# A transformer block with routed experts on one core: a new order of all sequences' steps, first weights on two queues, and a unit matrix transposed before the first operands

## The chip, the cores and the metric

The kernel runs on one core of a Trainium2 chip. A core has TensorE (matrix products, PE in the profile, with its weight loads as PEld), VectorE (DVE), ScalarE (ACT), GpSimd (POOL) and SyncE (SP), each with a queue of its own that is worked in order, and 16 DMA engines. The metric is the device time of one execution in microseconds, the median of the runs; lower is better.

## The reference: what is computed

All values are 32-bit floats. There are 16 sequences of 256 tokens of width 256. A conditioning vector per sequence is turned into a shift, then attention with 16 heads of width 64 runs, then eight experts each take the 512 tokens with the highest gate value.

```python
shift = silu(t) @ W_ada.T + b_ada
h = ln(x, ln1_g, ln1_b) + shift
qkv = (h @ Wqkv.T).reshape(b, n, 3, H, HD)
q = ln(qkv[:, :, 0].transpose(0, 2, 1, 3), qn_g, qn_b)
k = ln(qkv[:, :, 1].transpose(0, 2, 1, 3), kn_g, kn_b)
v = qkv[:, :, 2].transpose(0, 2, 1, 3)
attn = softmax(einsum('bhnd,bhmd->bhnm', q, k) / sqrt(HD))
x = x + einsum('bhnm,bhmd->bhnd', attn, v).transpose(0, 2, 1, 3).reshape(b, n, H * HD) @ Wout.T
tok = x.reshape(-1, d)
gate = softmax(tok @ Wgate.T)
vals, idx = top_k(gate.T, bs // E)
g = ln(tok[idx_flat], mlp_g, mlp_b).reshape(k_cap, E, d)
y = gelu(einsum('ked,ehd->keh', g, fc1s) + b1s)
y = (einsum('keh,edh->ked', y, fc2s) + b2s) * w[..., None]
tok = tok.at[idx_flat].add(y.reshape(-1, d))
```

## The kernel before, in words

**Tiles.** Tokens lie on the 128 partitions, two tiles to a sequence (t = 0, 1). A 32-bit matmul is two passes of TensorE, a transpose (a matmul against the unit matrix `ident`) is one, and the profile counts passes. The work of a sequence is cut into classes whose methods are *steps*:

- `First`: statistics of x on VectorE, a power of −1/2 on GpSimd (L82), normalised x (L500), four transposes (`ph`, L524), and the copy to `hT` with gain and shift on ScalarE (L532).
- `Group(g, t)`: 512 columns of the projection (`pm`, L556, two matmuls). Groups 0 and 1 make q, 2 and 3 make k, 4 and 5 make v. q and k groups then go through square (ScalarE, L569), sum (VectorE, L573), power (GpSimd), scale (VectorE, L589), four transposes (`pq`, L598) and a copy (ScalarE, L610); a v group is only copied (L565).
- `Quad(d)`: four heads, in two pairs i = 0, 1. Scores of a pair (`sc`, L631: four matmuls with 64 rows of operands), row maxima (VectorE, L638), exponentials with sums (ScalarE, L647), reciprocal, scaling (GpSimd, L658), transposes (`pp`, L667), copies to `prT` (VectorE L675 or ScalarE L677), the product with v (`po`, L685: four matmuls for a pair, each writing 64 rows of the result), and after both pairs one copy of `po` to `oT` (VectorE, L697).
- `Tail(t)`: the output projection (`pw`, L709, eight matmuls), residual, store, normalisation, the gate's logits (`pg` L731, `pl` L742).

**Routing and experts.** After the gates, a search of 30 steps finds each expert's threshold bit by bit: VectorE compares (L826), TensorE counts with two tiny matmuls (`pc`, L856 and L857), VectorE decides (L872). Then tokens get places (`pplace`), lists are made with one-hot matmuls (`pls`, L985), rows are gathered by indirect DMA, and 16 jobs (eight experts, two halves) run two matrix products each (L1032, L1048) and add their rows to the output by indirect DMA. The search for the first half runs while the last sequence's attention is under way.

**Buffers.** [...] three for tag `mm` (`pa`, `ph`, `pm`, `pq`, `pg` and small ones), four for `sc` (scores and the transposed exponentials), one for `po` (products, output projection, gate logits). In SBUF, `hT`, `qT`, `kT`, `v` and `oT` have two buffers each (the default of the pool, L426), x has five, `pr` and `prT` eight.

**What sets the order.** An engine works its instructions in the order in which the program issues them, and here that order is written out by hand as numbers. `at(places, *steps)` gives every step of every object a *place*; the whole plan is sorted by place and run once. Places of a sequence in the middle are those of `STEADY` plus b times `PERIOD`; `START` and `END` hold other places for the first and last sequences; `SHIFT`, `CENTER`, `GATES`, `TURN`, `SEARCH`, `PLACE`, `LIST`, `UP`, `DOWN` hold those of single steps. Places act by their order alone: nothing waits for a time. Of a step's instructions each goes to its own engine's queue. What follows the first job is issued by loops (`Job`, `lay_out`) outside the plan.

**The start.** SP issues the loads in this order: x of sequence 0, `wa`, the blocks of `wq` for groups 0, 2, 4, x of sequence 1, blocks 1, 3, 5, then `wo` (L465 to L472). `vec`, `cT` and `wg` go over ScalarE's queue. Blocks 0 to 3 are centred in place by VectorE before use (`center`, L478 to L480, twice per block).

Of the kernel before, what the change touches and what calls it, by code (L numbers as in the profile page):

```python
# [9 lines left out]
F32 = mybir.dt.float32  # L10
# [8 lines left out]
P = 128  # L19
# [24 lines left out]
def kernel(  # L44
# [35 lines left out]
    def rsqrt(dst, src):  # L80
# [59 lines left out]
    PERIOD = 55.74  # L140
    STEADY = dict(
        first=((-86.48, -78.84, -74.84), (-85.13, -84.23, -75.17), (-73.21, -72.54)),
        group={
            (0, 0): (-51.60, -49.66, -48.99, -47.86, -45.60, -40.27, -37.29),
            (0, 1): (-49.89, -47.94, -45.00, -43.96, -42.22, -32.07, -31.41),
            (1, 0): (-24.39, -22.45, -21.77, -20.73, -18.77, -16.60, -15.29),
            (1, 1): (-26.11, -24.16, -23.49, -22.45, -20.71, -11.67, -10.68),
            (2, 0): (-39.83, -37.89, -37.22, -36.18, -34.31, -31.64, -30.60),
            (2, 1): (-38.12, -34.68, -33.12, -32.08, -28.64, -21.80, -20.95),
            (3, 0): (-7.64, -4.23, -3.56, -1.89, 2.62, 3.70, 6.68),  # L150
            (3, 1): (-9.35, -7.41, -6.74, -3.55, -1.19, 9.31, 9.98),
            (4, 0): (-53.91, -51.13),
            (4, 1): (-42.15, -39.94),
            (5, 0): (-11.07, -8.97),
            (5, 1): (-4.61, -2.66),
        },
        quad={
            (0, 0): (0.00, 4.89, 9.75),
            (0, 0, 0): (1.42, 3.71, 5.16, 7.57, 8.23),
            (0, 0, 1): (2.02, 2.81, 6.07, 8.00, 8.67),  # L160
            (0, 1): (-1.04, 3.21, 12.60),
            (0, 1, 0): (0.23, 1.01, 6.97, 8.87, 9.54),
            (0, 1, 1): (0.83, 1.91, 3.48, 8.44, 9.26),
            (1, 0): (10.73, 16.50, 25.41),
            (1, 0, 0): (12.00, 12.78, 17.68, 19.77, 22.02),
            (1, 0, 1): (14.11, 14.89, 16.77, 19.33, 21.66),
            (1, 1): (11.77, 21.34, 28.26),
            (1, 1, 0): (15.91, 19.26, 22.51, 24.97, 25.74),
            (1, 1, 1): (14.71, 20.16, 21.61, 24.53, 25.95),
            (2, 0): (26.39, 30.55, 40.23),  # L170
            (2, 0, 0): (28.29, 29.37, 30.82, 33.50, 35.62),
            (2, 0, 1): (27.69, 28.47, 31.73, 34.37, 35.60),
            (2, 1): (27.43, 36.22, 43.08),
            (2, 1, 0): (29.48, 30.27, 37.58, 39.57, 40.24),
            (2, 1, 1): (28.88, 33.89, 36.67, 38.70, 39.86),
            (3, 0): (41.21, 45.50, 53.71),
            (3, 0, 0): (42.48, 43.26, 46.67, 50.69, 51.36),
            (3, 0, 1): (43.08, 44.16, 45.77, 50.25, 50.92),
            (3, 1): (42.25, 50.11, 56.57),
            (3, 1, 0): (44.90, 45.87, 51.28, 53.28, 53.94),  # L180
            (3, 1, 1): (45.58, 48.93, 50.38, 52.84, 53.67),
        },
        out=(15.31, 30.96, 44.30, 59.03),
        tail=((75.94, 79.63, 83.54, 87.30, 84.99, 86.37, 88.80, 89.54), (90.54, 94.23, 95.33, 101.91, 95.74, 99.41, 105.55, 106.29)),
# [3 lines left out]
            first=((-103.767, -95.871, -91.909), (-97.063, -91.499, -84.828), (-64.982, -60.069)),  # L188
            group={
                (0, 0): (-56.803, -54.747, -51.852, -46.726, -46.286, -40.948, -38.071),  # L190
                (0, 1): (-55.655, -51.889, -46.959, -45.652, -42.360, -35.597, -33.112),
                (1, 0): (-26.197, -24.462, -20.588, -19.209, -14.535, -13.716, -13.269),
                (1, 1): (-32.516, -25.059, -24.852, -21.979, -18.889, -16.671, -15.729),
                (2, 0): (-47.233, -46.547, -44.993, -44.096, -39.234, -33.671, -28.238),
                (2, 1): (-45.275, -40.554, -40.280, -39.778, -36.553, -34.586, -30.446),
                (3, 0): (-12.610, -11.185, -8.404, -8.124, -5.996, 0.834, 3.448),
                (3, 1): (-13.363, -12.739, -11.605, -8.322, -7.543, 0.483, 2.162),
                (4, 0): (-58.243, -54.205),
                (4, 1): (-38.500, -37.978),
                (5, 0): (-9.805, -0.465),  # L200
                (5, 1): (-0.114, 0.811),
            },
            quad={
                (0, 0): (-23.919, -5.908, 12.730),
                (0, 0, 0): (-18.292, -15.414, 1.499, 3.539, 11.030),
                (0, 0, 1): (-14.279, -11.333, -0.174, 4.332, 10.767),
                (0, 1): (-19.036, -1.502, 16.728),
                (0, 1, 0): (-15.547, -8.095, 3.988, 5.433, 14.399),
                (0, 1, 1): (-14.367, -13.775, 4.740, 9.194, 12.898),
                (1, 0): (-9.076, 3.092, 27.287),  # L210
                (1, 0, 0): (-6.911, -0.007, 10.749, 23.221, 26.164),
                (1, 0, 1): (-7.145, 1.038, 18.097, 23.303, 26.927),
                (1, 1): (-5.313, 10.835, 30.672),
                (1, 1, 0): (-5.048, 3.942, 10.903, 21.602, 24.260),
                (1, 1, 1): (-2.237, 6.984, 16.287, 26.090, 28.843),
                (2, 0): (14.616, 29.160, 50.712),
                (2, 0, 0): (18.721, 20.212, 39.985, 46.847, 48.427),
                (2, 0, 1): (17.079, 22.439, 35.099, 36.543, 39.030),
                (2, 1): (14.417, 20.717, 53.224),
                (2, 1, 0): (19.017, 20.432, 39.871, 41.557, 46.931),  # L220
                (2, 1, 1): (16.395, 19.203, 33.057, 36.198, 43.625),
                (3, 0): (28.358, 39.182, 56.816),
                (3, 0, 0): (33.283, 33.907, 42.060, 47.233, 48.706),
                (3, 0, 1): (30.676, 31.677, 45.808, 50.648, 52.914),
                (3, 1): (29.455, 40.685, 56.950),
                (3, 1, 0): (34.034, 35.650, 42.042, 47.065, 52.989),
                (3, 1, 1): (31.817, 31.879, 48.481, 49.433, 55.328),
            },
            out=(21.163, 46.372, 54.377, 59.310),
        ),  # L230
        1: dict(
            first=((-48.940, -38.543, -32.714), (-52.735, -35.719, -31.997), (-29.207, -15.966)),
            group={
                (0, 0): (2.354, 2.737, 3.370, 7.803, 9.249, 18.355, 19.310),
                (0, 1): (4.127, 4.691, 6.834, 9.818, 13.020, 18.898, 22.093),
                (1, 0): (24.336, 28.826, 29.227, 31.339, 32.252, 41.371, 43.504),
                (1, 1): (21.258, 24.606, 28.113, 28.269, 30.764, 34.230, 38.901),
                (2, 0): (5.363, 11.356, 12.710, 14.884, 17.055, 30.755, 32.598),
                (2, 1): (19.361, 21.502, 22.727, 23.222, 29.038, 44.181, 49.300),
                (3, 0): (46.783, 50.022, 51.249, 56.697, 57.141, 64.712, 66.361),  # L240
                (3, 1): (46.210, 46.527, 46.695, 49.934, 54.738, 57.230, 59.624),
                (4, 0): (-14.809, -14.323),
                (4, 1): (11.281, 14.349),
                (5, 0): (34.073, 38.872),
                (5, 1): (31.404, 35.141),
            },
        ),
        2: dict(
            first=((6.450, 29.164, 41.308), (24.474, 31.729, 34.174), (50.589, 52.650)),
        ),  # L250
    }
    SHIFT = (-80.440, (-78.087, -69.024), (-69.389, -63.749))
    CENTER = ((-57.472, -69.391), (-43.212, -34.432), (-52.040, -52.045), (-31.985, -38.697))
# [3 lines left out]
        12: dict(  # L257
            tail=((767.460, 778.446, 788.758, 796.220, 791.009, 793.004, 800.146, 803.267), (791.878, 796.704, 801.898, 813.493, 803.579, 805.200, 805.728, 806.788)),
        ),
        13: dict(  # L260
            quad={
                (0, 0): (722.824, 728.665, 740.826),
                (0, 0, 0): (727.159, 728.315, 730.472, 734.244, 735.366),
                (0, 0, 1): (727.038, 727.068, 730.471, 733.312, 740.658),
                (0, 1): (725.200, 732.291, 748.004),
                (0, 1, 0): (727.086, 728.457, 735.324, 738.809, 746.870),
                (0, 1, 1): (728.600, 728.974, 733.741, 737.090, 744.444),
                (1, 0): (746.975, 768.926, 788.232),
                (1, 0, 0): (753.635, 753.655, 772.854, 782.662, 785.291),
# [140 lines left out]
        dict(onehot=(1010.345, 1012.891, 1010.965,)),  # L410
    )
    UP = (
        (1006.088, 1008.000),
        (1008.282, 1008.303),
        (1008.002, 1008.011),
        (1009.875, 1011.434),
# [853 lines left out]
```

## Time and profile before

| what | value |
|---|---|
| median of 3 runs | 1201.21 us (1200.65 to 1202.83) |
| the profiled execution | 1200.95 us |
| its span, first to last instruction | 1199.2 us |
| TensorE busy | 1169.5 us |
| mean granted TensorE clock | 0.992 |
| row maxima, L638 | 256 of 681 ns |
| copy of po to oT, L697 (300 to 800 us) | 36 of 678 ns |
| power of a q or k group, L82 | 128 of 1650 ns |
| centring a block half, L478 to L480 | 0.68 + 0.17 + 0.69 us |

The profiled execution is one of its own, beside the runs of the median; the 1.75 us between its span and its time lie before the first and after the last instruction. A line of the timeline gives start, length, engine, source line, operation, operands and number of instructions; in brackets, idle time of the engine before it and what ended that. A matmul's length contains its latency, so neighbours overlap: the time that one takes out of TensorE's stream is the distance between starts.

### The profile page before, as it was taken

What the parts mean: (1) busy time and instruction counts of PE and PEld (TensorE: products, weight loads), DVE (VectorE), ACT (ScalarE), POOL (GpSimd) and SP (SyncE); (2) the same over time, 40 slices, a digit from 0 to 9 for tenths busy, and PEclk for the clock granted to TensorE, in tenths of its full rate; (3) what the DMA queues carried; (4) which work ended last, traced back from release to release, by engine and by line L of the source; (5) the groups of instructions that cost most, each with busy time, mean ns of one, the idle gap of its engine ahead of it and who ended that gap; (6) DMA issues with size and microseconds to landing.
All of it is one profiled execution on the core that took longest, in us unless ns stands there. A gap on an engine that the chain in (4) does not pass through costs nothing. (4 is left out here: it accounts for less than half of the span.)

```text
span 1199.2 us, 19564 instructions
## 1 busy us (share of the span) xinstructions
PE 1169.5 (98%) x6814; PEld 814.2 (68%) x6814; DVE 765.0 (64%) x2274; ACT 618.8 (52%) x1701; POOL 593.5 (49%) x820
## 2 busy tenths in 40 slices
PE   6999999999999999999999999999999899999996
PEld 3566666666675756666666666667755788888885
DVE  7666666657566657666666766665488567865541
ACT  2765565655556655555565655565575233333331
POOL 4564555555454555655555555555574333333332
PEclk9999999999999999999999999999999899999999
DMA  5000000000000000000001000000110366666661
GB/s 186 1 1 5 22 6 23 9 19 10 19 14 14 14 14 27 1 27 5 24 5 31 10 10 10 18 14 15 35 67 2 110 185 184 185 183 183 184 185 23
DMA packets 46738, 62.40 MB, mean 52 GB/s; under 512 B 3888, under 2 KB 39984, under 8 KB 46640
## 3 DMA queue, kind: packets, MB, share of 16 engines
q1 hardware_dynamic: 39808, 52.70, 13.1%
q0 software_dynamic: 6144, 8.39, 3.9%
q8 instruction: 54, 0.88, 0.3%
q14 instruction: 44, 0.36, 0.1%
q10 hardware_dynamic: 688, 0.06, 0.0%
HBM read 48.56 MB, written 12.58 MB: 51 GB/s over the span
## 5 line engine op out<-in xcount | busy, mean ns | idle before, releaser
L658 POOL TENSOR_SCALAR pr<-pr,sums 128x256 f32<-128x256 f32 x512 | 239.9, 489 | 265.1 <-DVE sums L654 252.0
L556 PE MATMUL pm<-wq,hT 128*128 128x512 f32 x768 | 357.5, 603 | 4.2 <-DMA wq<-in_wqkvT 2.7
L647 ACT ACTIVATE pr<-sc,nmax 128x256 f32<-128x256 f32 x512 | 236.5, 477 | 155.3 <-DVE nmax L638 154.8
L82 POOL TENSOR_TENSOR ss<-ss,neghalf 128x8 f32<-128x8 f32 x128 | 210.7, 1650 | 107.0 <-DVE ss L577 98.6
L556 PEld LDWEIGHTS pm<-wq,hT 128*128 128x128 f32 x768 | 137.6, 192 | 145.2 <-issue 134.0
L638 DVE TENSOR_REDUCE nmax<-sc 128x2 f32<-128x512 f32 x256 | 164.8, 681 | 43.4 <-PE sc L631 42.8
L573 DVE TENSOR_REDUCE ss<-sq 128x8 f32<-128x512 f32 x128 | 87.4, 683 | 107.1 <-ACT sq L569 107.0
L667 PEld LDWEIGHTS pp<-ident,pr 128*128 128x128 f32 x1024 | 118.3, 143 | 29.5 <-issue 18.3
L685 PE MATMUL po<-prT,v 128*64 128x256 f32 x1024 | 137.7, 391 | 0.1
L667 PE MATMUL pp<-ident,pr 128*128 128x128 f32 x1024 | 136.7, 274 | 0.0
L631 PE MATMUL sc<-kT,qT 64*128 64x256 f32 x1024 | 128.7, 390 | 0.0
L569 ACT ACTIVATE sq<-pm 128x512 f32<-128x512 f32 x128 | 77.1, 603 | 91.0 <-PE pm L556 89.4
L709 PE MATMUL pw<-wo,oT 128*128 128x256 f32 x512 | 119.1, 386 | 0.0
L1048 PE MATMUL py<-w,hid 128*128 128x256 f32 x512 | 119.0, 385 | 0.0
L1032 PE MATMUL ph<-xT,w 128*128 128x256 f32 x512 | 118.2, 383 | 0.0
L631 PEld LDWEIGHTS sc<-kT,qT 64*128 64x128 f32 x1024 | 93.4, 186 | 34.3 <-issue 23.6
L1058 POOL DMA_INDIRECT out<-y,idx x32 | 51.5, 1611 | 122.2 <-DVE y L1055 61.3
L709 PEld LDWEIGHTS pw<-wo,oT 128*128 128x128 f32 x512 | 96.7, 194 | 14.3 <-issue 1.2
L647 ACT ACTIVATION_READ_ACCUMULATOR pr<-sc,nmax 128x1 f32 x512 | 106.2, 207 | 0.0
L675 DVE COPY prT<-pp 128x512 f32<-128x512 f32 x112 | 76.9, 687 | 45.0 <-PE pp L667 44.7
L1048 PEld LDWEIGHTS py<-w,hid 128*128 128x128 f32 x512 | 96.1, 192 | 13.6
L1039 ACT ACTIVATE hid<-ph,vec 128x256 f32<-128x256 f32 x128 | 60.3, 474 | 85.8 <-PE ph L1032 74.4
(129 smaller groups left out, 1311.8 us busy)
## 6 DMA issues: line engine op xcount, KB each, us to landing
w<-in_fc2T SPq DMA_DIRECT2D x16, 1024.0 KB
w<-in_fc1T SPq DMA_DIRECT2D x16, 1024.0 KB
xs<-in_x SPq DMA_DIRECT2D x16, 256.0 KB
out<-tok SPq DMA_DIRECT2D x32, 128.0 KB
xn_dram<-tn SPq DMA_DIRECT2D x32, 128.0 KB
wq<-in_wqkvT SPq DMA_DIRECT2D x6, 512.0 KB
b<-in_b2s SPq DMA_DIRECT2D x16, 128.0 KB
wo<-in_woutT SPq DMA_DIRECT2D x1, 1024.0 KB
```

The source lines that it names most:

```text
L82: nc.gpsimd.tensor_tensor(dst, src, neghalf[:, : src.shape[1]], ALU.pow)
L556: nc.tensor.matmul(self.pm, hTs[self.b][:, c, bass.ts(self.t, P)], wq[:, c, bass.ts(self.g, GW)], start=(c == 0), stop=(c == DC - 1),)
L573: nc.vector.tensor_reduce(self.ss[:, 0, :], self.sq.rearrange("p (h d) -> p h d", d=HD), AX.X, ALU.add,)
L631: nc.tensor.matmul(self.sc[i, j][:, t, :], qTs[self.b][rows, hp, bass.ts(t, P)], kTs[self.b][rows, hp, :], start=True, stop=True,)
L638: nc.vector.tensor_reduce(self.nmax[i, j], self.sc[i, j], AX.X, ALU.max, negate=True)
L647: nc.scalar.activation(self.pr[i, j][:, t, :], self.sc[i, j][:, t, :], AF.Exp, bias=self.nmax[i, j][:, t : t + 1], scale=1.0, accum_out=se ...
L658: nc.gpsimd.tensor_scalar(self.pr[i, j][:, t, :], self.pr[i, j][:, t, :], self.sums[i][:, 1, j, t : t + 1], 1.0, ALU.mult, ALU.mult,)
L667: nc.tensor.transpose(self.pp[i, j][:, c, bass.ts(t, P)], self.pr[i, j][:, t, bass.ts(c, P)], ident,)
L685: nc.tensor.matmul(self.po[j * HD : (j + 1) * HD, i, :], vs[self.b][:, c, bass.ts(4 * self.d + 2 * i + j, HD)], self.prT[i, j][:, c, :], s ...
L709: nc.tensor.matmul(self.pw, oTs[self.b][:, hp, bass.ts(self.t, P)], wo[:, hp, :], start=(hp == 0), stop=(hp == HP - 1),)
L1032: nc.tensor.matmul(self.ph[f], self.w1[:, c, bass.ts(f, P)], self.xT[:, c, :], start=(c == 0), stop=(c == DC - 1),)
L1048: nc.tensor.matmul(self.py[i], self.hid[:, f, bass.ts(i, P)], self.w2[:, f, :], start=(f == 0), stop=(f == FC - 1),)
```

## The change

All places are replaced: `PERIOD`, `STEADY`, `START`, `END` and the single lists. `START` now has places of its own for more of sequences 0 to 3. In `STEADY`, the two products of a quad (third number of a `(d, i)` entry) get neighbouring places, later than before, so that they follow each other without other work between them. In TensorE's order of a middle sequence, runs of `po x4, sc x8, po x4` become `sc x8, po x8` (twice), `po x8, sc x8, po x8` (once) and `sc x8` alone (once). The tag `v` gets three buffers in place of two, also where an expert's weights use it.

The first loads: SP issues x of sequence 0, `wa`, and the `wq` blocks 4, 0, 2. The other five loads (x of sequence 1, blocks 1, 3, 5, `wo`) go over ScalarE's queue as a step of the plan whose place is just after the copies to `hT`. On SP, the loads of x for sequences 2 and 3 follow at once.

Twenty transposes of `ident` into a PSUM tile that nobody reads are new: 16 as TensorE's first instructions, four after the first sequence's `ph` transposes. On VectorE the two instructions of `bias` (L459) now stand ahead of all centrings.

```diff
-    PERIOD = 55.74
+    PERIOD = 55.238
...
-            (0, 0): (0.00, 4.89, 9.75),
+            (0, 0): (0.000, 6.254, 13.508),
...
-            (0, 1): (-1.04, 3.21, 12.60),
+            (0, 1): (-1.059, 4.018, 13.509),
...
-            (1, 0): (10.73, 16.50, 25.41),
+            (1, 0): (11.585, 16.798, 31.441),
...
-            (1, 1): (11.77, 21.34, 28.26),
+            (1, 1): (12.644, 23.095, 31.442),
...
+    LOADS = -61.203
...
-        def load_x(b):
+        def load_x(b, queue=nc.sync):
             xs[b] = seq.tile([P, TB, D], F32, tag="xs", bufs=5, name=f"xs{b}")
-            nc.sync.dma_start(
+            queue.dma_start(
...
+        def warm(n):
+
+            for _ in range(n // 4):
+                pt = ps.tile([P, GW], F32, tag="sc", bufs=4, name="warm")
+                for i in range(4):
+                    nc.tensor.transpose(pt[:, bass.ts(i, P)], ident, ident)
...
-        for g in (0, 2, 4, 1, 3, 5):
-            nc.sync.dma_start(wq[:, :, bass.ts(g, GW)], wq_dram[:, :, bass.ts(g, GW)])
-            if g == 4:
-                load_x(1)
-        nc.sync.dma_start(wo, woutT.rearrange("(h p) d -> p h d", p=P))
+
+        def load_wq(g, queue):
+            queue.dma_start(wq[:, :, bass.ts(g, GW)], wq_dram[:, :, bass.ts(g, GW)])
+
+        for g in (4, 0, 2):
+            load_wq(g, nc.sync)
+
+        def later_loads():
+            load_x(1, nc.scalar)
+            for g in (1, 3, 5):
+                load_wq(g, nc.scalar)
+            nc.scalar.dma_start(wo, woutT.rearrange("(h p) d -> p h d", p=P))
...
-                tiles[b] = seq.tile(shape, F32, tag=tag, name=f"{tag}{b}")
+                tiles[b] = seq.tile(
+                    shape, F32, tag=tag, bufs=3 if tag == "v" else 2, name=f"{tag}{b}"
+                )
...
-                self.w1 = seq.tile([P, DC, DD], F32, tag="v", name="w1")
+                self.w1 = seq.tile([P, DC, DD], F32, tag="v", bufs=3, name="w1")
...
+        turn = places(0)["first"][TB][0]
+        at((turn - 50.0, turn + 0.001), partial(warm, 16), partial(warm, 4))
         at(SHIFT[:1], shift.silu)
+        at([LOADS], later_loads)
...
-                at([its["first"][0][0] - 20.0], partial(load_x, b))
+                at([min(its["first"][t][0] for t in range(TB)) - 20.0], partial(load_x, b))
```

## The prediction, made before the changed kernel ran

> **What bounds the kernel now.** I read the page's busy shares first, then the same shares by stage, then TensorE's timeline in the three places where the stages differ. The page's first part and the windows view (length of the stretch, then busy time of each engine with its number of instructions, granted clock, DMA share) say:
>
> ```profile
> PE 1169.5 (98%) x6814; PEld 814.2 (68%) x6814; DVE 765.0 (64%) x2274; ACT 618.8 (52%) x1701; POOL 593.5 (49%) x820
> ```
> ```profile
> 0.00:20.00 20.00, 12.02 (x28) 6.16 (x28) 12.30 (x32) 4.20 (x7) 7.04 (x22) 1.00 0.85 279
> 20.00:40.00 20.00, 16.48 (x63) 8.23 (x62) 15.75 (x34) 8.30 (x13) 10.02 (x8) 0.91 0.00 0
> 40.00:880.00 840.00, 840.00 (x4792) 549.91 (x4791) 539.15 (x1228) 494.69 (x1431) 456.41 (x663) 1.00 0.05 17
> 880.00:900.00 20.00, 17.20 (x101) 9.95 (x101) 18.00 (x83) 14.88 (x44) 16.98 (x26) 1.00 0.00 0
> 920.00:940.00 20.00, 17.49 (x114) 12.59 (x111) 15.44 (x75) 2.06 (x5) 8.75 (x12) 0.83 0.05 14
> ```
>
> The reader is to see that TensorE does not stop once between 40 and 880 us. There a time is saved only by taking time out of TensorE's own stream; no other engine matters as long as it is not late (VectorE, the fullest, has 539 of 840 us). Idle TensorE time exists at the start (20 − 12.02 + 20 − 16.48 = 11.5 us), around the routing search from 880 to 960 us (2.80 + 1.32 + 2.51 + 1.73 = 8.4 us over the four windows of 20 us) and after the last matmul (1189.4 to 1199.2 us, 9.8 us).
>
> The start, TensorE's timeline (start, length, engine, line, what, and the idle time before it with what ended it):
>
> ```profile
> 5.12 1.89 PE L453 MATMUL pa<-sT,wa 128*128 128x16 f32 x8 [5.12 <-ACT sT L448]
> 11.06 9.51 PE L556 MATMUL pm<-wq,hT 128*128 128x512 f32 x16 [2.70 <-DMA wq<-in_wqkvT]
> 25.91 3.57 PE L556 MATMUL pm<-wq,hT 128*128 128x512 f32 x4 [0.87 <-ACT qT L610]
> ```
> ```profile
> 14.61 0.33 PEld L556 LDWEIGHTS pm<-wq,hT 128*128 128x128 f32 x1 [0.52 <-issue]
> 15.46 0.33 PEld L556 LDWEIGHTS pm<-wq,hT 128*128 128x128 f32 x1 [0.52 <-issue]
> 16.55 0.19 PEld L556 LDWEIGHTS pm<-wq,hT 128*128 128x128 f32 x1 [0.24 <-issue]
> 16.98 0.19 PEld L556 LDWEIGHTS pm<-wq,hT 128*128 128x128 f32 x1 [0.24 <-issue]
> ```
>
> The first projection waits for the third block of weights, and until about 16 us one pass of 512 columns takes 0.85 us (14.61 to 15.46), after it 0.43 (16.55 to 16.98). So TensorE runs at half speed there, although the windows view shows 1.00. At 25.91 us four passes take 3.4 us again, after a stretch with gaps: half speed once more.
>
> The steady part, TensorE's timeline twice: one quad of a steady sequence, and places where the same matmuls already stand together:
>
> ```profile
> 607.08 1.08 PE L685 MATMUL po<-prT,v 128*64 128x256 f32 x8
> 608.09 2.00 PE L631 MATMUL sc<-kT,qT 64*128 64x256 f32 x16
> 610.02 1.08 PE L685 MATMUL po<-prT,v 128*64 128x256 f32 x8
> 611.03 1.98 PE L556 MATMUL pm<-wq,hT 128*128 128x512 f32 x4
> ```
> ```profile
> 87.73 1.95 PE L685 MATMUL po<-prT,v 128*64 128x256 f32 x16
> 89.61 2.00 PE L631 MATMUL sc<-kT,qT 64*128 64x256 f32 x16
> 91.54 1.95 PE L685 MATMUL po<-prT,v 128*64 128x256 f32 x16
> 93.41 0.66 PE L598 MATMUL pq<-ident,qk 128*128 128x128 f32 x4
> ```
>
> From start to next start, eight passes of a product cost 1.01 us, sixteen in one run 1.88 (87.73 to 89.61). Two runs of eight cost 2.02, so each pair put together is worth 0.15 us (2 x 1.014 − 1.877 with the third digit of the starts).
>
> [...] a product uses 64 columns of the array, scores 64 rows, and every separate run of products carries those 0.15 us. [...]
>
> **The change, part by part.**
>
> *Products.* Counted in TensorE's order of instructions before and after: before, 123 runs of products, 118 of them of four matmuls (eight passes); after, 64 runs, all of eight matmuls. Entries into the 64-wide modes from ordinary matmuls stay (77 and 75), and in a steady sequence the exits do too. That is 59 joined pairs, 4 of them in the last sequence, inside the search, where TensorE has spare time. 55 x 0.15 = 8.25 us. Against it, scores of one pair of heads that are cut off alone: 6 such runs before, 10 after; two halves cost 2 x 1.07 against 1.93, and two or three of the new ones lie outside the search: 0.2 us. Net 8.0 us, which is 0.60 us in each of the steady periods of 56.2 us.
>
> *What hides the delay of products.* They now come up to 18 us after the last transposed copy instead of about 1 us. For this v gets a third buffer; without it the next sequence's v would wait. The product's only PSUM bank is now used twice around one run of scores (products, scores, products: once per sequence). Between them VectorE must copy it: 0.68 us (row of L697, 678 ns) in the 1.93 us of the scores, so 1.25 us of slack less the handover. At 87.73 the same triple stands already and shows no idle. Cost 0; if VectorE had more than 1.2 us of other work ahead of it, the excess would be paid once per sequence.
>
> *Start.* Bias (two instructions, L459) now stands on VectorE before the centring, so it can run at 7.62 (end of xn) instead of 9.06, and hT at the end of the transposes, 8.4 instead of 9.44. The v block, which needs no centring, is loaded first and lands where the first block does now (before 7.54, when its centring began). So the first projection can begin at about 10.0 instead of 11.06: 1.0 us. The q projection then needs centred weights: second block about 9, two centrings of 1.55 us, about 12.2; before it began at 14.5 (four passes of 0.85 after 11.06). With a fast clock the group would run 12.2 to 13.9 and the first scaled qk would come 2.3 us earlier than 20.49, since VectorE still has four centrings to about 15.3 us ahead of the statistics; with a slow clock about 1.1 us earlier. The 16 transposes of ident start at 1.6 (ident ready at 1.53 on POOL) and at twice the steady 0.109 us end about 5.1, when the first real matmul gets its operand: cost 0 to 0.2. The other four lie in the wait for hT. For the half-speed stretch at 25.9 (1.7 us lost) I take a 40% chance that it goes, 0.7 us. Sum of the start: 1.1 to 2.3, plus 0.7: 2.5 us; bounds 0.5 and 5.
>
> *Issues moved to ScalarE.* x1, three blocks of wq and wo: on SP such issues took 0.37 us (x, wo) and 0.5 to 0.9 (wq). On ScalarE, between hT and the first square: 0.74 + 3 x (0.5 to 0.9) = 2.2 to 3.4 us, so until 11.7 to 12.9. The first square has no operand before 13.9. Hidden. SP, now free, issues x2 and x3 earlier; they put 0.5 MB, some 1.5 us at the 340 GB/s of the DMA view, before the late blocks. The first of these is used by a centring at about 18 us and lands about 15.5. Hidden; uncovered it would be a few us once.
>
> *Search and end.* Between its first and last count the search has 26.4 us of TensorE filler before and 27.0 after, but placed less evenly: steps with only four transposes (0.44 us) go from ten to 15, against about 1.05 us for the shortest step (counts at 891.11 and 892.16). VectorE's other work in it grows from 30.5 to 31.2 us. By the larger of the two per step, idle grows by about 1 us; after the search the filler ahead of the lists grows by 0.7 us. I take 0.3 us lost, bounds −1.5 and +2. The expert stage and the last 9.8 us are unchanged.
>
> **Sum.** 8.0 + 2.5 − 0.3 = 10.2 us. The profiled execution took 1200.95 (span 1199.2 and 1.75 around it): 1190.75. The median of the runs lies 0.26 above it: **1191.0 us**.
>
> **Rivals.**
> - *The forecast* (60%): 1188.5 to 1193.5.
> - *More at the start* (15%): transposes do warm the clock, both half-speed stretches go and part of the 3.5 idle us from 20 to 40; start 5 to 6, total 13 to 14, 1187. For: the idle is there; against: VectorE is 79% busy there and the gaps are its waits.
> - *The new order is a little late each sequence* (18%): it was laid out for a period 0.50 us shorter (its own constants, 55.74 to 55.238), not 0.60; and small waits of 0.1 to 0.5 us per sequence over 13 sequences give back 1.3 to 6.5 us: 1192 to 1197.5. Against: before has none in 840 us.
> - *Slower* (5%): the bank copy between two product runs comes late every time. It decides from 10.2/13 = 0.78 us of wait per sequence, which needs 1.25 + 0.78 = 2.0 us of VectorE work (three instructions of 0.68) between the first run's end and its copy. At 1.2 us per sequence: 1191 + 15.6 = 1206.6. Against: the triple at 87.73, and in VectorE's order the copy directly follows two copies of prT that can end before the products do.
> - *No net effect* (2%): the same wait at about 0.75 us.
>
> **How the numbers follow.** A measurement tells 0.2% (2.4 us) from no change. Faster is the first three cases, 0.93; same 0.02; slower 0.05. The range takes the forecast, most of the richer start and most of the third case: 1185.5 to 1196.5.
>
> **What would show it.** In the profile of after: 16-pass runs of products of 1.88 us, a period of about 55.6 us between transposes of neighbouring sequences, and still 840 busy of 840 us; first projection at about 10 us; passes of 0.43 us from the first projection on if transposes warm the clock, from 14 to 17 us if not. Wrong would be any wait of TensorE that recurs with the period (on VectorE's copy of po above all), or a search with several us more of idle.

## The result, and the profile after

The changed kernel takes 1194.72 us in the median (1193.51 to 1197.12; one execution at 4552.94 us stands apart and is left out) against 1201.21: a ratio of 0.9948, 95% interval 0.9932 to 0.9963, so 4.4 to 8.2 us less. The forecast was 1191.0, which is 10.2 us less. The profiled execution is the slowest of the four, 1197.12 us with a span of 1195.2.

The same two views of the changed kernel as shown of the kernel before, busy shares and then the windows (length, busy time of TensorE, weight loads, VectorE, ScalarE and GpSimd, granted clock, DMA share, GB/s):

```profile
PE 1164.6 (97%) x6834; PEld 819.7 (69%) x6834; DVE 759.5 (64%) x2274; ACT 624.6 (52%) x1701; POOL 591.0 (49%) x820
```
```profile
0.00:20.00 20.00, 14.99 (x46) 8.98 (x47) 10.29 (x28) 3.85 (x7) 7.28 (x22) 0.83 0.84 279
20.00:40.00 20.00, 16.91 (x65) 8.42 (x64) 17.59 (x38) 10.79 (x22) 9.25 (x8) 1.00 0.01 1
40.00:880.00 840.00, 839.48 (x4833) 556.28 (x4832) 542.65 (x1258) 505.43 (x1442) 463.11 (x677) 1.00 0.05 17
880.00:900.00 20.00, 17.75 (x120) 11.19 (x120) 16.95 (x89) 13.52 (x41) 12.05 (x20) 1.00 0.00 1
920.00:940.00 20.00, 16.80 (x119) 14.03 (x118) 14.72 (x81) 5.14 (x9) 9.39 (x12) 0.83 0.38 125
```

TensorE is still busy throughout 40 to 880 us (839.48 of 840), so the new order is hardly ever late there. The start has more work and less idle. Its clock is given as 0.83 where before has 1.00, but the 1.00 leaves out the half speed of before, which by its passes of 512 columns (0.85 us, then 0.43) lasted until about 16 us.

Windows at fixed times compare different work once one kernel is ahead. So I add up TensorE's passes, each at its steady duration in the profile of before (0.430 us for 512 columns, 0.216 for 256, 0.120 for scores, 0.117 for products in one run, 0.109 for a transpose), 1124.6 us in all, and note when each profiled execution has done the same sum. The difference to the kernel before, in us:

| profiled execution | at 40 us of work (the start) | at 820 (search begins) | at 870 (search done) | at 900 (second job's rows used) | at 1080 (experts) |
|---|---|---|---|---|---|
| changed kernel | −1.1 | −8.4 | −7.5 | −9.9 | −4.1 |
| changed kernel, run again | −5.1 | −12.3 | −11.5 | −14.0 | −8.6 |

Both profiles gain 7.3 us between 40 and 820, lose 0.9 in the search, gain 2.4 to 2.5 from there to 900, and then give back 5.4 to 5.8. They differ in the start alone. The column at 40 can shift by some 0.4 us with where in a pass the sum is met, and the column at 870 by some 0.5 us with what the search's tiny matmuls are counted at, in all changed kernels alike; so the 7.3 is 6.9 to 7.3, and the split of search and after is rough.

The gain before 900 is at the second expert job. TensorE's timeline there, of the kernel before and of the changed kernel:

```profile
949.35 0.30 PE L1013 MATMUL px<-ident,xg 128*128 128x128 f32 x1 [1.56 <-DMA xg<-xn_dram,idx]
...
950.83 5.31 PE L1048 MATMUL py<-w,hid 128*128 128x256 f32 x16
```
```profile
941.91 0.90 PE L1075 MATMUL px<-ident,xg 128*128 128x128 f32 x4 [0.34 <-DMA xg<-xn_dram,idx]
942.64 3.62 PE L1110 MATMUL py<-w,hid 128*128 128x256 f32 x16
```

The wait for the gathered rows falls from 1.56 to 0.34 us, and the 16 passes after it no longer begin at half speed (3.62 us for 5.31; in the kernel before the granted clock is 0.50 from 951.17 to 954.58 us). Together that is 2.9 us, of which the stage keeps 2.4 to 2.5.

What is given back after 900 is seen in the view of waits of the changed kernel (who waits for what, us in total, times, longest) and in TensorE's timeline:

```profile
PE px L1075 <- DMA xg<-xn_dram,idx: 4.2, 2, 3.9
PE pc L919 <- DVE reach L888: 4.0, 14, 0.5
PE pm L618 <- DVE wq L540: 2.9, 1, 2.9
PE pls L1047 <- POOL oh L1038: 2.8, 5, 0.7
```
```profile
967.29 0.78 PE L1075 MATMUL px<-ident,xg 128*128 128x128 f32 x4 [3.86 <-DMA xg<-xn_dram,idx]
967.91 3.47 PE L1110 MATMUL py<-w,hid 128*128 128x256 f32 x8
```

The top wait is new: the rows gathered for the third expert job come 3.86 us late. After it, eight passes of 256 columns take 3.27 us from start to start (967.91 to the next at 971.18) where eight cost 1.73 at full speed: TensorE has fallen to half speed (the granted clock is 0.50 from 968.06 to 971.47 us), which costs 1.5 us by the passes and 1.7 by half of that stretch. GpSimd's and SP's timelines of the changed kernel show why the rows are late:

```profile
951.31 1.67 POOL L1120 DMA_INDIRECT out<-y,idx  x1 [11.50 <-DVE y L1117]
959.90 1.57 POOL L1120 DMA_INDIRECT out<-y,idx  x1 [6.93 <-DMA out<-y,idx]
...
963.26 1.05 POOL L1066 DMA_INDIRECT xg<-xn_dram,idx  x1
964.61 0.99 POOL L1066 DMA_INDIRECT xg<-xn_dram,idx  x1 [0.30 <-issue]
```
```profile
950.19 0.38 SPq L1010 DMA_DIRECT2D w<-in_fc2T  x1
950.63 0.57 SPq L1012 DMA_DIRECT2D w<-in_fc1T  x1
```

The first job's result is added to the output by two scatters (L1120), the second of which waits for the first to land. The first is issued at 951.31, 1.1 us after SP began to issue 2 MB of weights. It lands 7.8 us later, and the gather (L1066), behind both in GpSimd's queue, goes out only at 963.26. In the kernel before, the first scatter went out ahead of the weights and landed after 3.9 us; GpSimd's and SP's timelines:

```profile
957.28 1.66 POOL L1058 DMA_INDIRECT out<-y,idx  x1 [11.34 <-DVE gates L748]
```
```profile
960.06 0.38 SPq L948 DMA_DIRECT2D w<-in_fc2T  x1
```

The cause lies in the last line of the plan: before, the half i = 1 was finished (`finish`, two VectorE instructions) at place 1019.361, between the two down projections at 1014.649 and 1020.447; in the changed kernel it is finished at 1057.278, after both (1047.604 and 1056.315). That is a theory until it is tried.

### The profile page after: what moved, and what is told of

Same layout as the page of the kernel before. It is cut to its first block, busy times and chain, and to the rows that moved or that the text cites. A ratio compares the mean times of both kernels' runs of the same rounds, so it can differ in the third digit from the quotient of the medians.

```text
span 1195.2 us, 19652 instructions
## 1 busy us (share of the span) xinstructions
PE 1164.6 (97%) x6834; PEld 819.7 (69%) x6834; DVE 759.5 (64%) x2274; ACT 624.6 (52%) x1701; POOL 591.0 (49%) x820
## 5 line engine op out<-in xcount | busy, mean ns | idle before, releaser
L618 PE MATMUL pm<-wq,hT 128*128 128x512 f32 x768 | 364.8, 605 | 4.7 <-DVE wq L540 2.9
L720 POOL TENSOR_SCALAR pr<-pr,sums 128x256 f32<-128x256 f32 x512 | 236.9, 481 | 208.9 <-DVE sums L716 162.2
L618 PEld LDWEIGHTS pm<-wq,hT 128*128 128x128 f32 x768 | 134.7, 192 | 129.0 <-issue 112.9
L747 PE MATMUL po<-prT,v 128*64 128x256 f32 x1024 | 124.6, 385 | 0.0
L1120 POOL DMA_INDIRECT out<-y,idx x32 | 51.5, 1609 | 123.7 <-DVE y L1117 73.1
L1110 PEld LDWEIGHTS py<-w,hid 128*128 128x128 f32 x512 | 95.8, 192 | 13.5
L1094 PEld LDWEIGHTS ph<-xT,w 128*128 128x128 f32 x512 | 95.3, 191 | 13.4
```

Of the source, the lines that this page charges most:

```text
L618: nc.tensor.matmul(self.pm, hTs[self.b][:, c, bass.ts(self.t, P)], wq[:, c, bass.ts(self.g, GW)], start=(c == 0), stop=(c == DC - 1),)
L720: nc.gpsimd.tensor_scalar(self.pr[i, j][:, t, :], self.pr[i, j][:, t, :], self.sums[i][:, 1, j, t : t + 1], 1.0, ALU.mult, ALU.mult,)
L747: nc.tensor.matmul(self.po[j * HD : (j + 1) * HD, i, :], vs[self.b][:, c, bass.ts(4 * self.d + 2 * i + j, HD)], self.prT[i, j][:, c, :], s ...
L1094: nc.tensor.matmul(self.ph[f], self.w1[:, c, bass.ts(f, P)], self.xT[:, c, :], start=(c == 0), stop=(c == DC - 1),)
L1110: nc.tensor.matmul(self.py[i], self.hid[:, f, bass.ts(i, P)], self.w2[:, f, :], start=(f == 0), stop=(f == FC - 1),)
```

## The experiments

Ratios are to the kernel before on the same chip, with 95% intervals. Where I speak of stages, the table of equal work is meant; the rows of the experiments are gathered below.

**The changed kernel once more**

> The changed kernel once more, as the base of the three beside it. Both theories: 1193 to 1196 us, 0.994 to 0.996 of the kernel before. If the late gather of the third expert job varies from run to run, TensorE's wait for it (3.9 us in the first profile, at 967.3 us) can be anything from 1 to 5 us here.

1193.15 us, 0.9938 (0.9923 to 0.9953). The profile's wait for the third job's rows is 2.69 + 0.65 us, in two pieces. Loss between 900 and 1080: 5.4 us, as in the first profile within 0.4. This profile is the base for the stages below.

**The first job's result finished early**

```diff
-    DOWN = ((1056.315, 1057.008), (1047.604, 1057.278))
+    DOWN = ((1056.315, 1057.008), (1047.604, 1048.900))
```

> The second half of the first expert job's result is finished (two VectorE instructions) right after its own down projection, as in the kernel before, and its scatter is placed there too. Theory: in the changed kernel the first scatter is issued at 951.3 us behind the 2 MB of weights issued at 950.2, the second waits for it until 959.9, and the gather of the next job comes behind both; with the scatter some 4 us ahead of the weights the gather is issued about 4 us earlier, the wait of TensorE for the gathered rows (3.9 us) falls below 1 us, and so does the half-speed stretch after it (1.7 us): 2.5 to 5.5 us less than the changed kernel. Rival (the gather is late for another reason, such as the slower search or the list matmuls before it): within 1 us of the changed kernel, the wait stays.

1189.32 us, 0.9900 (0.9885 to 0.9916), 3.8 us below the run above, and the intervals are apart. GpSimd's timeline, and TensorE's at the third job:

```profile
942.87 1.67 POOL L1120 DMA_INDIRECT out<-y,idx  x1 [8.01 <-DVE y L1117]
947.54 1.57 POOL L1120 DMA_INDIRECT out<-y,idx  x1 [3.00 <-DMA out<-y,idx]
950.95 1.19 POOL L1066 DMA_INDIRECT xg<-xn_dram,idx  x1 [0.41 <-DVE chunk L1020]
```
```profile
958.34 0.64 PE L1075 MATMUL px<-ident,xg 128*128 128x128 f32 x4
958.82 1.89 PE L1110 MATMUL py<-w,hid 128*128 128x256 f32 x8
```

The second scatter now follows 4.67 us after the first, not 8.59; the gather is 7.4 us ahead of its use, TensorE does not wait (no bracket), and the eight passes take 1.72 us. Nothing is given back between 900 and 1080 (−14.82 and −14.81). The theory holds, the rival falls.

**The kernel before with the late finish**

```diff
-    DOWN = ((1020.447, 1020.575), (1014.649, 1019.361))
+    DOWN = ((1020.447, 1020.575), (1014.649, 1020.700))
```

> The kernel before, with the second half of the first expert job's result finished only after the other down projection, as the changed kernel does it; nothing else. Theory (this alone makes the third job's gather late): the first scatter moves from ahead of the weight load to behind it, TensorE waits 2.5 to 4 us for the gathered rows and then runs at half speed for one stretch: 3.5 to 6 us slower than the kernel before. Rival (the kernel before has slack here that the changed kernel lost through its other moves): within 1 us of the kernel before.

1206.97 us against 1198.67, 1.0064 (1.0050 to 1.0079). The one number makes the old kernel lose what the new one lost, and more than expected: 8.3 us in the medians and 6.9 in the stage, for 3.5 to 6. TensorE's timeline, then GpSimd's:

```profile
976.44 0.30 PE L1013 MATMUL px<-ident,xg 128*128 128x128 f32 x1 [3.98 <-DMA xg<-xn_dram,idx]
977.71 0.90 PE L1013 MATMUL px<-ident,xg 128*128 128x128 f32 x3 [0.97 <-DMA xg<-xn_dram,idx]
```
```profile
960.33 1.66 POOL L1058 DMA_INDIRECT out<-y,idx  x1 [15.22 <-DVE y L1055]
970.24 1.60 POOL L1058 DMA_INDIRECT out<-y,idx  x1 [8.24 <-DVE cand L845]
```

The scatter falls 1.1 us behind the weights (SP issued them from 959.22), as in the changed kernel; the two waits are 3.98 and 0.97, and half speed follows (the next eight passes, from 978.41 us, take 3.03 us to the start of what follows, for 1.73). The stage loses 6.9 us.

**Products parted again**

```diff
-            (1, 0): (11.585, 16.798, 31.441),
+            (1, 0): (11.585, 16.798, 29.400),
...
-            (2, 0): (29.518, 34.134, 56.102),
+            (2, 0): (29.518, 34.134, 54.100),
```

> In the steady sequences the products of the second and third quad are parted again around a run of scores: 22 runs of products more, nothing else moved. Theory (each parting costs about 0.15 us of TensorE's own time): 22 x 0.15 = 3.3 us more than the changed kernel. Rival (the joins were worth less, and the period fell for the other moves of the order): under 1.5 us more, and a period above 55.75 us only by 0.1.

1194.31 us, 0.9950 (0.9936 to 0.9965): only 1.2 us above the changed kernel in the median, which by itself would speak for the rival, although each of the two ratios is known to no better than 1.8 us. The stage says otherwise: from 40 to 820 it gains 3.9 us where the changed kernel gains 7.3. 3.3 us are lost, 0.15 for each of the 22 joins, and the period is 55.99 against 55.69. In the profiled executions 1.5 us of them come back after the list. TensorE's timeline there, the first line from the changed kernel run again, the second from the kernel with parted products:

```profile
920.50 7.54 PE L771 MATMUL pw<-wo,oT 128*128 128x256 f32 x20
```
```profile
923.89 6.02 PE L771 MATMUL pw<-wo,oT 128*128 128x256 f32 x20
```

The same 20 passes take 1.5 us less. At full speed they take 4.56 us (at 917.46 in the run with the list, below), so some 2.9 us of them ran at half speed here and 6.0 there, an estimate of twice what is above 4.56. So a total can hide a cost of this size, and a stage shows it.

**Without the transposes of ident**

```diff
-        at((turn - 50.0, turn + 0.001), partial(warm, 16), partial(warm, 4))
```

> The 20 transposes of the unit matrix are left out, the rest is the changed kernel. Theory (TensorE waits for the centred weights of the query block in any case, and the clock that the transposes raise is lost in that wait): within 0.7 us of the changed kernel; the granted clock is still low at 8 us, the first projection starts at 8.3 to 9 us and takes twice as long, and the query projection still starts at about 12.9. Rival (the early clock is what the start gained): 1.5 us or more slower than the changed kernel.

1193.33 us, 0.9934 (0.9918 to 0.9949): no difference to the changed kernel. TensorE's timelines at the start, the changed kernel's first profile and then the run without the transposes:

```profile
1.58 3.68 PE L493 MATMUL warm<-ident 128*128 128x128 f32 x16 [1.58 <-POOL ident masks.py:199]
...
8.10 1.96 PE L618 MATMUL pm<-wq,hT 128*128 128x512 f32 x4 [0.43 <-DMA wq<-in_wqkvT]
12.95 8.48 PE L618 MATMUL pm<-wq,hT 128*128 128x512 f32 x12 [2.89 <-DVE wq L540]
```
```profile
8.40 3.67 PE L618 MATMUL pm<-wq,hT 128*128 128x512 f32 x4 [0.66 <-ACT hT L592]
13.15 5.42 PE L618 MATMUL pm<-wq,hT 128*128 128x512 f32 x12 [1.09 <-DVE wq L540]
```

With the transposes the first projection runs at full speed (1.96 us for four passes against 3.67), but in this execution TensorE then stands 2.89 us for the centred weights of q and falls back (granted clock 0.50 from 12.33 to 19.15 us): 12 passes take 8.48 us. Without them TensorE is busy until 12 us at half speed, waits 1.09, and the 12 passes take 5.42. What the transposes brought to this execution was lost again in its wait for q.

Nor do they bring it every time. The eight passes of `pa` that come next take 0.98 to 1.43 us in five of the eight profiles with transposes, but 1.89 in the three others (early finish, two edits, two edits and the list), as without transposes (1.86). In those three the first projection begins at half speed, too: its 16 passes take 7.83 to 8.24 us, where 16 of 0.430 are 6.9. TensorE's timeline of the early finish:

```profile
1.58 3.67 PE L493 MATMUL warm<-ident 128*128 128x128 f32 x16 [1.58 <-POOL ident masks.py:199]
...
9.01 7.83 PE L618 MATMUL pm<-wq,hT 128*128 128x512 f32 x16
```

Yet these three gain the most at the start, 5.2 to 5.6 us (last table of this section).

**The old order of loads**

```diff
-        for g in (4, 0, 2):
+        for g in (0, 2, 4, 1, 3, 5):
             load_wq(g, nc.sync)
+            if g == 4: load_x(1)
...
-            load_x(1, nc.scalar)
-            for g in (1, 3, 5):
-                load_wq(g, nc.scalar)
-            nc.scalar.dma_start(wo, woutT.rearrange("(h p) d -> p h d", p=P))
+            pass
+        nc.sync.dma_start(wo, woutT.rearrange("(h p) d -> p h d", p=P))
```

> The changed kernel with the first weights loaded as in the kernel before: blocks in the order 0, 2, 4, 1, 3, 5, x of the second sequence after the third, all and the output weights on SP. Theory A (the new places of the first sequences make most of what the start gained, about 5 us in the runs whose weights came in time): the first projection starts at about 11 us instead of 8 to 9, and at 100 us of TensorE work 0.5 to 2 us of the gain are lost. Theory B (the order of loads makes it): 3 us or more are lost.

1194.79 us, 0.9968 (0.9953 to 0.9984). The first projection starts at 10.46 us, and at 40 us of work 1.1 us are gained where the changed kernel run again had 5.1: 4.0 us lost, the size of theory B. In TensorE's timeline both half-speed stretches are there as before the change (granted clock 0.54 from 8 to 12 us, 0.61 from 12 to 16, 0.67 from 24 to 28):

```profile
10.46 9.41 PE L618 MATMUL pm<-wq,hT 128*128 128x512 f32 x16 [1.76 <-DMA wq<-in_wqkvT]
...
25.19 3.66 PE L618 MATMUL pm<-wq,hT 128*128 128x512 f32 x4 [0.87 <-ACT qT L672]
```

One profile does not carry the 4.0: the changed kernel's first profile, with the new loads, gained only 1.1 us too. What holds in every profile is the second stretch. Behind the wait for `qT` (0.87 us), the four passes of the next projection take 3.57 to 3.66 us in all three executions with the old loads (before, before with the late finish, and this one) and 1.98 to 1.99 in all eight with the new. The ratios put the whole loss at 2.4 to 3.6 us (0.9968 against 0.9948 and 0.9938), with an interval that overlaps that of the changed kernel's first measurement, so the sign is likely and the size open. The edit undoes two things at once, the order of the blocks and the queue of the other five loads; their shares are not shown.

**Three edits, and what each does**

```diff
-        for g in (4, 0, 2):
+        for g in (0, 4, 2):
...
-        tail=((75.024, 80.051, 81.151, 92.875, 82.383, 82.831, 90.365, 92.705), (97.967, 101.653, 107.912, 115.175, 104.452, 104.900, 115.900, 117.411)),
+        tail=((75.024, 80.051, 81.151, 92.875, 82.383, 82.831, 90.800, 92.705), (97.967, 101.653, 107.912, 115.175, 104.452, 104.900, 116.350, 117.411)),
```

with the early finish as above.

> Three edits of the changed kernel, each read in its own stage. The early finish of the first job's result: no loss at the third job's gather, as when it was made alone. The query block's weights loaded first and the value block's second: centring starts at about 7.5 us in every run instead of 8.2 to 9.9, so the scaled queries come 0.7 to 2.4 us earlier than in the changed kernel; rival: the first projection waits for the value block until 9 to 10 us and gives that back, 0. In the steady sequences each gate projection of 8 columns is moved behind the projection that followed it, so that transposes follow it as in the kernel before: theory (a 512-wide projection right after it costs 0.08 us, transposes 0.03) the period falls by 0.10 from 55.67 to 55.57 us; rival: it stays. Sum: 1187 to 1190 us.

1186.53 us, 0.9898 (0.9881 to 0.9915), a little below the sum expected. Early finish: nothing given back after 900, again. Query block first: centring starts at 8.02 us, not at 7.5, the first projection waits for the value block until 9.52, and 4.3 us are gained at 40 us of work against 5.1; the rival holds. It also shows that most of the gain at the start does not need the value block to come first. Gate projections moved: the period falls from 55.69 to 55.59. TensorE's timelines, the changed kernel and then this one:

```profile
399.70 0.51 PE L804 MATMUL pl<-wg,tokT 128*128 128x8 f32 x4
400.07 1.96 PE L618 MATMUL pm<-wq,hT 128*128 128x512 f32 x4
401.87 1.47 PE L729 MATMUL pp<-ident,pr 128*128 128x128 f32 x12
```
```profile
397.84 0.51 PE L804 MATMUL pl<-wg,tokT 128*128 128x8 f32 x4
398.21 1.51 PE L729 MATMUL pp<-ident,pr 128*128 128x128 f32 x12
399.55 1.88 PE L618 MATMUL pm<-wq,hT 128*128 128x512 f32 x4
```

A projection right after the 8-column gate takes 1.80 us from start to start instead of 1.72, while transposes after it take 0.03 more; twice in a period that is the 0.10.

**Two edits, and the list**

The run with two edits has the early finish and the moved gates, with the changed kernel's own loads. The last adds:

```diff
-                engine = nc.gpsimd if a is jobs[0] and k in (2, 5) else nc.vector
+                engine = nc.gpsimd if a is jobs[0] and k in (2,) else nc.vector
```

> The early finish and the moved gate projections, with the changed kernel's own order of loads (value block first). Theory: the order of loads of the run before bought nothing, so this is as fast or faster: no loss at the third job's gather, period 55.58 to 55.60, 1185 to 1188.5 us. If the query block first had helped, this would be 1 to 2 us slower than the run with three edits.

> As the run with two edits, and five of the ten comparisons that GpSimd makes for the first expert job's list go to VectorE. GpSimd takes 0.67 us for each and ends at about 924.2 us in the profile of the changed kernel, VectorE takes 0.18 us and ends its 25 at 922.5. Theory (TensorE's 2.8 us of waits before the list are those on GpSimd): VectorE ends at about 923.4, the list is complete 0.5 to 0.8 us earlier: 0.5 to 1 us less. Rival: VectorE is the limit just as well: no gain.

1186.39 us, 0.9889 (0.9872 to 0.9906), and 1183.40 us, 0.9860 (0.9840 to 0.9880). The list's waits, TensorE's timeline of the first and then of the second:

```profile
916.20 0.18 PE L1047 MATMUL pls<-give,oh 128*128 128x10 bf16 x1 [0.70 <-POOL oh L1038]
...
918.85 0.59 PE L1047 MATMUL pls<-give,oh 128*128 128x10 bf16 x16 [0.40 <-POOL oh L1038]
```
```profile
916.64 0.96 PE L1047 MATMUL pls<-give,oh 128*128 128x10 bf16 x10 [0.80 <-DVE oh L1038]
```

The first is within its expectation; the second is 3.0 us lower where 0.5 to 1 was expected, though the two intervals still overlap a little. Five waits, 2.62 us in all, become one of 0.80, so the list ends 1.8 us earlier. Half speed after it lasts 3.4 us in place of 6.8 (granted clock 0.83 from 920 to 930 us, against 0.84 from 915 to 920 and 0.74 from 920 to 930), which is worth 1.7 us more. TensorE then waits 0.78 us for `tok` and 0.42 us for gathered rows, which takes part of it back, and the profiles differ by 2.1 us in the end. What the list is worth without the change of the clock was not separated. This is the fastest kernel of the study, 1.4% under the kernel before.

The stages of all profiled executions, difference to the kernel before in us:

| kernel | at 40 | at 820 | at 900 | at 1080 |
|---|---|---|---|---|
| early finish | −5.6 | −12.9 | −14.8 | −14.8 |
| before, late finish | −0.8 | −0.8 | −0.9 | +6.1 |
| products parted | −5.0 | −8.9 | −12.1 | −7.0 |
| without transposes | −3.9 | −11.1 | −13.1 | −7.4 |
| old loads | −1.1 | −8.3 | −10.2 | −4.3 |
| three edits | −4.3 | −12.6 | −15.1 | −15.1 |
| two edits | −5.2 | −13.5 | −15.3 | −15.3 |
| two edits and the list | −5.2 | −13.5 | −17.4 | −17.4 |

## Why the prediction was right, and where it was not

The side and the range were right; the time was 3.7 us off, because several terms of the sum missed, and in part cancelled. That part is luck: in the repeated profile the start brought 2.6 us more than counted and the second job's rows 2.5, against 5.4 lost at the third job's.

- *Products joined, 8.0 us, 0.60 a period.* The price of a join is shown: 22 joins undone cost 3.3 us. The period fell by 0.50. The missing 0.10 are the gate projections, which the new order puts ahead of 512-wide projections; I compared only entries into and exits from the 64-wide modes. Moving them gives the 0.10 back. The rival "a little late each sequence" had named 0.50 a period: its figure came true, its reason, recurring waits, did not. From 40 to 820 us of work 7.3 us are gained, and 8.3 with the gates moved.
- *The delay of products costs nothing.* Right: 839.48 of 840 us busy, no wait that recurs.
- *Start, 2.5 us, bounds 0.5 and 5.* Mis-sized: 1.1 us in the first profile, 5.0 to 5.6 in the five others whose start is that of the changed kernel. By its size this was the rival "more at the start". I took the transposes not to raise the clock, an assumption that no trace of the kernel before shows; here they can: in the changed kernel run again the eight passes right behind the 16 transposes, from 4.99 us, take 0.98 us against 1.86 without transposes, and in the first profile the first projection takes 0.49 us a pass with its latency against 0.92. The measurement decides, though in three of eight profiles it did not happen. And they are not what made the gain, as their removal shows. The loads have a part in it, since with the old ones a half-speed stretch returns; the size of that part, 4.0 us in one profile and 2.4 to 3.6 by the ratios, is open. The first projection came at 7.9 to 9.0 us, not 10.0, and the 40% chance for the half-speed stretch at 25.9 was too low: it is gone in every profile with the new loads. In the first profile the q block landed late (centring began at 9.75 us, against 8.76 when run again, 8.21 with the early finish and 8.69 with the products parted), the wait reached 2.9 us, and the clock was 0.50 for the next 6.8 us.
- *Issues moved to ScalarE.* Right: they end at 10.3 us in the first profile, and the first square has its operand only at 14 to 17 us.
- *Search, 0.3 us lost, bounds −1.5 and +2.* 0.9 us are lost by the table: a size, within the bounds.
- *"The expert stage and the last 9.8 us are unchanged."* This is the step that failed, on both sides: 2.4 to 2.5 us are gained up to the second job's rows and 5.4 to 5.8 lost at the third's. The end did stay as it was (9.8 us after the last matmul), but from the unchanged code of the jobs I concluded that their order against the queues of SP and GpSimd was unchanged too. `DOWN` was in the change, and the finish of the half i = 1 had moved behind the other half's down projection. Two runs, one in each direction, show that this alone is the loss. What made the second job's rows come earlier was not tried. In the traces GpSimd issues that gather 3.4 us behind a job's weights before and 4.3 us behind them after the change, and TensorE has the rows 6.5 and 5.4 us after the issue; whether the shorter distance is why the rows took longer before is not shown.

With the repeated profile the sum is 5.1 + 7.3 − 0.9 + 2.5 − 5.4 = 8.6 us, against 10.2 forecast.

## What to carry to other kernels

When a plan of places is rewritten, compare every queue's order around each DMA whose landing someone waits for, GpSimd's scatters and gathers too: here a small scatter that fell 1.1 us behind a 2 MB load took twice as long to land (7.8 us for 3.9), and the scatter and the gather behind it in its queue came late. Price a stall on TensorE with the half-speed stretch that may follow it (here 1.7 or 3.4 us, half of the 3.41 or 6.83 us that a stretch lasted). And compare runs at equal work, stage by stage; the total of one execution hid here about half of a cost of 3.3 us.

## What the runs showed that I had not expected

An indirect write of 128 rows landed late when it was issued just behind a job's weights, and not only at the first job. In the changed kernel's first profile, 14 of the 32 scatters were issued 1.1 to 2.0 us after SP had begun to issue 2 MB of weights, and landed 7.0 to 8.8 us after their own issue. The 18 others, at least 9.7 us behind, landed after 3.8 to 4.0 us. The first job's first scatter landed at 959.12 us there, the last of the weights at 958.95.

In the profiles of the kernel before and of the changed kernel, TensorE's half-speed stretches between two of full speed are 3.41 or 6.83 us long. Which one it was, no edit set: after nearly the same waits for the list (0.70, 0.50, 0.50, 0.53 and 0.40 us in the changed kernel run again, 0.69, 0.50, 0.50, 0.53 and 0.40 with the products parted) the next 20 passes took 7.54 and 6.02 us. In each of these two profiles the changes of the granted clock lie on one grid of 3.41 us. In the changed kernel's first they are at 12.33, 19.15, 923.68, 930.51, 968.06, 971.47 and 1189.92 us, which is 2, 265, 2, 11, 1 and 64 steps from one to the next; in the kernel before at 26.16, 29.57, 930.69, 937.52, 951.17, 954.58 and 1193.52 us, 1, 264, 2, 4, 1 and 70 steps. Counted in whole steps back from the first of these, the grid lies 2.09 us and 2.27 us after the kernel's start. A wait need not be long: in the kernel before a half-speed stretch follows one of 1.56 us (at 949.35), while in the changed kernel run again a wait of 2.10 us for the weights of q (until 11.96) cost no clock (the 12 passes after it took 5.42 us, for 8.48 in the first profile). What decides between them is not shown.

Transposes of 32-bit data alone brought the clock to full speed in the changed kernel run again: 3.4 us after the first of them (1.58), the eight passes from 4.99 us take 0.98 us. And a 512-wide projection after an 8-column matmul costs 0.08 us more than after a wide one (1.80 us for four passes against 1.72), which nothing in the table of busy times tells.
